# Query norm in the copy of x, attention's sums for two tiles at once, and a reordered schedule, in a fused convolution and linear-attention kernel

## The chip, the core and the metric

The kernel runs on one core of a Trainium2 chip. The metric is the device time of one execution in microseconds (us), the median of several runs. The engines are named as in the profile: PE (matrix products, with PEld for its weight loads), DVE (vector), ACT (scalar), POOL (GpSimd) and SP (the queue that issues the DMAs here). Each engine executes its own instructions in the order in which the program lists them.

## What is computed

There are 16 images x of 256 channels and 64 by 64 pixels, all in float32. For each image:

```python
x = x + conv(gn(x)) * mod        # gn: group norm, 32 groups; conv: 3x3, 8 groups of 32 channels,
                                 # its taps rotated by angles that are computed from the image
t = gn(x)                        # the second norm, as tokens: 4096 x 256
q = t @ Wq.T + bq ; k, v = split(t @ Wkv.T + bkv)
q = (relu(q) + 1e-6) / scale ; k = (relu(k) + 1e-6) / scale
q = q**3 / |q**3| * |q| ; k = k**3 / |k**3| * |k|
z = 1 / (q . sum(k) + 1e-6)                        # 8 heads of 32
out = q @ (k.T @ v) * z + depthwise5x5(v)
x = x + out @ Wproj.T + bproj
```

## The kernel before

**Phases of one image.** The whole order is written out by hand for every engine (a manual schedule). In the key phase (`key_step`, n = 2 to 15 for all but the first image) each step makes 256 tokens' keys and values: `key_products` (PE, L588), `key_bias` (DVE), `squares` (ACT, sums of squares for the focusing norm), `cube` (POOL, L567), `ratio` (DVE) and `root` (POOL, L576), `key_scale` (ACT, L608), and `values`, which adds k.T @ v into PSUM (PE, L621). `key_store` writes the values to DRAM and `load_blocks` reads them back as 12 by 8 blocks (`vh`) for the depthwise convolution. Sixteen such loads fill `vh` for the upper half of the image, the last two being issued after n = 14. `depthwise` (PE `pd`, L658, with ACT copying `pd` into `fm`) needs all sixteen.

`between` is the transition: the first two `query_products` (PE `pq`, L683), the last three `values`, and the depthwise convolution of the upper half.

Then come 17 steps of `attention_step`, p = 1 to 17. In step p, `turn` transposes the queries of group p-1 (PE `pt`, L698; ACT copies `pt` to `qT`, L703), `query_products` makes group p+1, `query_bias` adds bias and relu on DVE (L557, L558), `turn_back` transposes the output of group p-2 (PE `po`, L734; ACT copies it to `oT`), `attend` makes the sums of group p-1 (PE `pn`, L715) and `project` multiplies group p-2 by Wproj (PE `py`, L744). `add_up` (DVE, L756) adds the result to x one step later. On PE a step thus runs `pt`, `pq`, `po`, `pn`, `py`. In `attend` DVE makes the denominators `zz` (L717), inverts them (L720) and multiplies (`o`, L724), and POOL adds the depthwise result (`o`, L726), each for two tiles j = 0, 1 in turn; `po` of the next step reads `o`.

**What is laid over the attention steps.** The next image's 3x3 convolution runs in the same steps: `convolve` (PE `pc`, four PSUM banks) at the end of p = 2, 3, 4 and 9, 10, 11, in parts A, P, B. In the step after it `evict` empties the four banks q = 0 to 3 into x (part A on ACT, P on ACT and DVE, B on DVE). `settle` corrects the edges of x (POOL, L443) and then takes the statistics for the second norm (DVE, L444). The lower half's depthwise convolution is in p = 9. `norm1` is the second norm of the next image, a chain whose links are stepped through one at a time by `next(chain)`: bn_aggr on DVE; `pm` (PE, L196) and four small DVE instructions; `pv` (PE, L203), `vs` (DVE, L205) and a power on POOL (L206); `fold_scale`, which multiplies Wkv by the norm's factor (DVE, L531); `fold_shift`, which subtracts the mean's part from the bias (PE `pbkv`, L538, and DVE). Two links per step are made, from p = 14, one in the middle and one at the end. The next image's first keys are made in p = 16 and 17.

**What sets the order around the change.** Each engine's queue is what is written in these functions. PSUM has six banks in a ring (`bank`, L90): a product waits until the bank taken six before it has been read. Two more banks hold k.T @ v, and later the sums of the two tiles. The tables say in which step something happens:

```python
SETTLES = {4: (0, 0, (0, 1), (2, 3)), 8: (0, 1, (0,), ()), 9: (0, 1, (1, 2), (3,)),
           11: (1, 0, (0, 1), (2, 3)), 13: (1, 1, (0, 1), ()), 14: (1, 1, (2, 3), ())}
```

(step: half, row parity, the quarters settled in the middle of the step, those settled late in it.) Wq is treated as Wkv is: loaded again for each image, scaled by the norm (`fold_scale(b, "q")` at n = 5) and its bias corrected (`fold_shift(b, "q")` at n = 8, PE `pbq`). `blocked` (ACT, L675) copies x into the token order of a query group.

Of the kernel before, what the change touches and what calls it, by code (L numbers as in the profile page):

```python
# [26 lines left out]

STRIP = 2 * ROWS
# [8 lines left out]
SETTLES = {4: (0, 0, (0, 1), (2, 3)), 8: (0, 1, (0,), ()), 9: (0, 1, (1, 2), (3,)),  # L37
           11: (1, 0, (0, 1), (2, 3)), 13: (1, 1, (0, 1), ()), 14: (1, 1, (2, 3), ())}
# [6 lines left out]
STATS = {1: (0,), 2: (1, 2), 3: (3,), 7: (4,), 9: (5, 6), 10: (7,)}  # L45
# [18 lines left out]
def conv_attention(ctx: ExitStack, tc: tile.TileContext, x, consts, kw, b1, w2, b2, b2r,  # L64
# [16 lines left out]
    ps = pool("ps", 6, space=PSUM)  # L81
# [7 lines left out]

    def bank(name):  # L90
        return ps.tile([P, CH], F32, tag="bank", name=name)
# [7 lines left out]
    def load_stats(b, i):  # L99
        if i == 0:  # L100
            state[b] = {"x": {}, "k": {}, "xs": {},
                        "st": sp.tile([P, 2, NCH, 6], F32, tag="st0", name=f"st0_{b}", bufs=1)}

            if b > 1:
                state[b]["xw"] = wsp.tile([P, 2, CH], F32, tag="wkv", name=f"xs_{b}")
        if b > 1:
            xt = state[b]["xw"]
            for t in range(2):
                nc.sync.dma_start(xt[:, t, :], x[b, ts(t, P), ts(i, CH)])
        else:  # L110
            xt = xp.tile([P, 2, CH], F32, tag="x", name=f"xs_{b}_{i}")
            nc.sync.dma_start(xt, halves(x[b])[:, :, ts(i, CH)])
        state[b]["xs"][i] = xt

    def take_stats(b, i):
        xt = state[b]["xs"].pop(i)
        for t in range(2):
            nc.vector.bn_stats(state[b]["st"][:, t, i, :], xt[:, t, :])
# [66 lines left out]
    def gn_coefs(st, b, which):  # L185


        mv = sp.tile([P, 2, 2], F32, tag="mv", name=f"mv{which}_{b}")
        for t in range(2):
            nc.vector.bn_aggr(mv[:, t, :], st[:, t])  # L190
        yield
        mean, var = mv[:, :, 0], mv[:, :, 1]
        co = sp.tile([P, 5, 2], F32, tag=f"co{which}", name=f"co{which}_{b}")
        a, pooled, d, v, m = (co[:, k, :] for k in range(5))
        pm = bank(f"pm{which}_{b}")[:, 0:2]
        nc.tensor.matmul(pm, lhsT=g8, rhs=mean, start=True, stop=True)  # L196
        nc.vector.tensor_copy(m, pm)
        nc.vector.tensor_sub(d, mean, m)
        nc.vector.tensor_mul(v, d, d)
        nc.vector.tensor_add(v, v, var)  # L200
        yield
        pv = bank(f"pv{which}_{b}")[:, 0:2]
        nc.tensor.matmul(pv, lhsT=g8, rhs=v, start=True, stop=True)  # L203
        vs = sp.tile([P, 2], F32, tag="vs", name=f"vs{which}_{b}")
        nc.vector.tensor_scalar(vs, pv, EPS_GN, None, ALU.add)  # L205
        nc.gpsimd.tensor_tensor(a, vs, mhalf, ALU.pow)  # L206
        yield
        if which == 0:
            nc.vector.tensor_mul(pooled, d, a)
        return a, pooled, m  # L210
# [7 lines left out]
    def prepare(b):  # L218
# [15 lines left out]
        nc.vector.tensor_add(h, ph, b1_t)  # L234
        nc.vector.tensor_scalar(h, h, 0.0, None, ALU.max)
# [14 lines left out]
        nc.vector.tensor_add(mod, pmod, b2r_t)  # L250

# [9 lines left out]
        nc.vector.tensor_copy(edge, pe)  # L261
        state[b]["edge"] = edge
# [61 lines left out]
        def shifts(t):  # L324


            pb = bank(f"pbias_{b}_{t}")[:, 0:3]
            for j in range(4):
                for dx in range(3):
                    nc.tensor.matmul(pb[ts(j, HD), dx:dx + 1], lhsT=sums[t][:, dx, :], rhs=gm[:, t, j:j + 1],  # L330
                                     start=True, stop=True, tile_position=(0, HD * j))
            nc.vector.tensor_copy(shift[:, t, 0:3], pb)
            nc.vector.tensor_reduce(shift[:, t, 3:4], shift[:, t, 0:3], AX.X, ALU.add)
            nc.vector.tensor_scalar(shift[:, t, 3:4], shift[:, t, 3:4], -1.0, None, ALU.mult)
# [84 lines left out]
    def evict(b, u, part, q):  # L419

        at, shift = (2 * u + q // 2, q % 2), state[b]["shift"][:, q % 2, 3:4]
        pc = state[b]["pc"][q].rearrange("p (r w) -> p r w", w=W)
        fresh = at not in state[b]["x"]
        if fresh:
            state[b]["x"][at] = xp.tile([P, 2 * CH], F32, tag="x", name=f"x_{b}_{at[0]}_{at[1]}")
        rows = rows_16(b, u, q)
        if part == "P":
            nc.scalar.activation(rows[:, 1], pc, AF.Identity, bias=shift, scale=-1.0)
        if part == "B":
            nc.vector.tensor_add(rows[:, 1], pc, rows[:, 1])  # L430
        elif fresh:
            nc.scalar.activation(rows[:, 0], pc, AF.Identity, bias=shift)
        else:
            nc.vector.tensor_add(rows[:, 0], pc, rows[:, 0])  # L434

# [72 lines left out]
    nc.vector.tensor_add(bp_t, bp_t, pb)  # L508

# [23 lines left out]
    def fold_shift(b, name):  # L533
# [6 lines left out]
        nc.vector.tensor_sub(br, br, pb[:, 0:n])  # L540

    def norm1(b):
        a, _, m = yield from gn_coefs(state[b]["st1"], b, 1)
        state[b]["gn1"] = (a, m)
        fold_scale(b, "kv")
        yield
        fold_shift(b, "kv")
# [44 lines left out]
    def key_bias(b, n, j):  # L592
# [4 lines left out]
        nc.vector.tensor_add(vbuf[n % NV][:, j, 0:HD, :].rearrange("p c h -> p (c h)"), pm[:, C:2 * C], br[:, C:2 * C])  # L597

# [11 lines left out]
    def values(b, n):  # L610


        if n == 0:
            state[b]["pkv"] = [psk.tile([P, HD + 1], F32, tag=f"kv{hh}", name=f"pkv{hh}_{b}") for hh in range(2)]
# [33 lines left out]
    def depthwise(b, half, c):  # L648
# [7 lines left out]
        for k in range(4):  # L656
            for j in range(4):
# [8 lines left out]
                       pd.rearrange("p k (T h) -> p k T h", h=NH))  # L666


    def blocked(b, m):
# [3 lines left out]
        for t in range(2):  # L673
            xt = chunk(b, i, t).rearrange("p (y R J c) -> p R J y c", y=BR, R=2, c=BC)
            nc.scalar.copy(xq[:, t, :].rearrange("p (J y c) -> p J y c", y=BR, c=BC), xt[:, R])  # L675
        state[b]["xq"][m] = xq

    def query_products(b, m):
        xq, (w, _) = state[b]["xq"].pop(m), state[b]["q"]
# [9 lines left out]
    def query_bias(b, m):  # L689
        f = state[b]["f"][m]  # L690
        relu(f["r"], f["pq"], state[b]["q"][1].unsqueeze(1).to_broadcast([P, 2, C]))
# [9 lines left out]
    def turned(b, m):  # L701
        qT = op.tile([P, 2, 2, P], F32, tag="qT", name=f"qT_{b}_{m}", bufs=1)
        nc.scalar.copy(qT, state[b]["pt"])  # L703
        state[b]["qT"] = qT

    def attend(b, m):
# [4 lines left out]
        pns = []  # L711
        for j in range(2):
            pn = psk.tile([P, HD + 1, NH], F32, tag=f"kv{j}", name=f"pn_{b}_{m}_{j}")
            for hh in range(2):
                nc.tensor.matmul(pn[:, :, 4 * hh:4 * hh + 4], lhsT=qT[:, hh, j, :], rhs=kvx[:, hh],  # L715
                                 start=True, stop=True)
            nc.vector.scalar_tensor_tensor(z[:, j, :], factor[:, j:j + 1].to_broadcast([P, NH]), EPS, pn[:, HD, :],  # L717
                                           ALU.mult, ALU.add)
            pns.append(pn)
        nc.vector.reciprocal(z, z)  # L720
        state[b]["o"] = []
        for j in range(2):
            o = op.tile([P, HD, NH], F32, tag="o", name=f"o_{b}_{m}_{j}")
            nc.vector.tensor_mul(o, pns[j][:, 0:HD, :], z[:, j, :].unsqueeze(1).to_broadcast([P, HD, NH]))  # L724
            o = o.rearrange("p c h -> p (c h)")
            nc.gpsimd.tensor_add(o, o, fm[:, 2 * (m % NCH) + j, :])  # L726
            state[b]["o"].append(o)

    def turn_back(b, m):

        po = bank(f"po_{b}_{m}").rearrange("p (t j n) -> p t j n", t=2, j=2)
        for j in range(2):
            for t in range(2):
                nc.tensor.transpose(po[:, t, j, :], state[b]["o"][j][:, ts(t, P)], ident)  # L734
        oT = op.tile([P, 2, 2 * P], F32, tag="oT", name=f"oT_{b}_{m}", bufs=1)
        nc.scalar.copy(oT.rearrange("p t (j n) -> p t j n", j=2), po)  # L736
        state[b]["oT"] = oT
# [14 lines left out]
    def add_up(b, m):  # L752
        i, R = divmod(m, 2)
        for co in range(2):
            xt = chunk(b, i, co).rearrange("p (y R n) -> p R y n", y=BR, R=2)[:, R]
            nc.vector.scalar_tensor_tensor(xt, state[b]["py"][:, co], bp_t[:, co:co + 1], xt, ALU.add, ALU.add)  # L756

# [62 lines left out]
    def between(b, more):  # L820
# [7 lines left out]
        query_bias(b, 0)  # L828
        key_scale(b, NP - 2)
        blocked(b, 2)  # L830
        squares(k[NP - 1], 1)
        for n in range(NP - LATE, NP - 2):
            values(b, n)
        query_products(b, 1)
# [4 lines left out]
        values(b, NP - 2)  # L839
        query_bias(b, 1)  # L840
        for c in range(0, HD // 2, 4):
            depthwise(b, 0, c)
        key_scale(b, NP - 1)
# [10 lines left out]
    def attention_step(b, p, chain):  # L854
# [7 lines left out]
        v, s, early, late = SETTLES.get(p, (0, 0, (), ())) if more else (0, 0, (), ())  # L862
# [3 lines left out]
        if part:  # L866
            evict(b + 1, u, part, 0)
        if p >= 3:
            add_up(b, p - 3)
            store(b, p - 3)  # L870
        if p - 1 < NP:
            turn(b, p - 1)
            turned(b, p - 1)
        if part:
            evict(b + 1, u, part, 1)
# [5 lines left out]
        for q in early:  # L881
            settle(b + 1, v, s, q)
        if chain:
            next(chain, None)
        if p == NP + 1:
            turn_back(b, p - 2)
        if n >= 0:
# [6 lines left out]
            if n >= 1:  # L894
                squares(k[n - 1], 0)
                cube(k[n - 1])
            key_bias(b + 1, n, 0)
            key_bias(b + 1, n, 1)
        if part:
            evict(b + 1, u, part, 2)  # L900
# [9 lines left out]
        for q in late:  # L910
            settle(b + 1, v, s, q)
# [12 lines left out]
        if p >= 2:  # L924
            project(b, p - 2)
        if more and p in SUMS:
# [3 lines left out]
        if chain:  # L930
            next(chain, None)
# [12 lines left out]
    with tc.manual_schedule():  # L944
        fold_load(0, "q")
        made = iter(())
        for b in range(B):
            more = b + 1 < B
            state[b]["f"], state[b]["xq"] = {}, {}
            for n in range(0 if b == 0 else LEAD, NP):  # L950
# [12 lines left out]
                if b > 0 and n == LEAD:  # L963
                    fold_load(b, "q")
                if n == 5:
                    fold_scale(b, "q")
                if n == 8:
                    fold_shift(b, "q")
# [99 lines left out]
```

## Time and profile before

| | |
|---|---|
| median of 3 runs | 3654.27 us (3651.45 to 3654.44) |
| the profiled execution | 3651.46 us, of which its span is 3649.7 us |
| PE busy | 3425.5 us, 94% of the span |
| PEld, DVE, ACT, POOL busy | 71%, 68%, 56%, 56% |
| mean granted PE clock | 0.984 |
| DMA | 505.90 MB, 139 GB/s on average |

All numbers are of one execution. A row of the page or of the groups names the line, the engine, the operation, out<-in with shapes and the count; then the busy time and the mean of one in ns; then the engine's idle time just before these instructions and what ended it. A row of the timeline gives start and length in us, and in brackets the idle time before it and its releaser. Idle time of an engine that isn't the bottleneck costs nothing by itself.

### The profile page before, as it was taken

The numbers are of one execution on the slowest core, as the hardware profiler recorded it, in microseconds if no ns is written. First come the engines' busy times: TensorE is split into PE (matmuls) and PEld (weight loads), VectorE is DVE, ScalarE is ACT, GpSimd is POOL, SyncE is SP. The second block draws the span as 40 slices with busy tenths as digits, with TensorE's granted clock in tenths as the row PEclk, the third lists the DMA queues.
The fourth block names the chain that finished last, engine by engine and source line by source line (L and its number), as shares of the span: only waits on it lengthen the run. The fifth ranks groups of instructions, "written<-read, shape, count | busy, mean of one in ns | idle before, by whom it ended". The sixth has DMA issues, their size and how long they took to land. (4 is left out here: it accounts for less than half of the span.)

```text
span 3649.7 us, 109597 instructions
## 1 busy us (share of the span) xinstructions
PE 3425.5 (94%) x43496; PEld 2580.0 (71%) x43496; DVE 2477.9 (68%) x6627; ACT 2036.9 (56%) x6501; POOL 2034.4 (56%) x2554
## 2 busy tenths in 40 slices
PE   2799999999999999999999999999999999999999
PEld 1467677677777767776677776777777776777778
DVE  4667767667676666766677576776766667676656
ACT  2264654647556465564646546475564755646565
POOL 4265555556555565564655555565555655546545
PEclk8899999999999999999999999999999999999999
DMA  4263552635436253462634526355262534525242
GB/s 138 95 196 102 155 164 76 201 95 171 153 103 203 80 180 122 131 180 82 204 107 154 164 69 209 95 167 158 96 206 85 180 121 139 175 80 182 78 145 99
DMA packets 191173, 505.90 MB, mean 139 GB/s; under 512 B 30742, under 2 KB 103960, under 8 KB 178373
## 3 DMA queue, kind: packets, MB, share of 16 engines
q1 hardware_dynamic: 190660, 498.89, 43.4%
q8 instruction: 344, 5.64, 0.7%
q14 instruction: 169, 1.38, 0.1%
HBM read 363.24 MB, written 135.53 MB: 137 GB/s over the span
## 5 line engine op out<-in xcount | busy, mean ns | idle before, releaser
L588 PE MATMUL pk<-wkv,x 128*128 128x512 f32 x2048 | 951.6, 611 | 0.0
L588 PEld LDWEIGHTS pk<-wkv,x 128*128 128x128 f32 x2048 | 617.5, 310 | 213.2 <-issue 6.1
L726 POOL TENSOR_TENSOR o<-o,fm 128x256 f32<-128x256 f32 x512 | 365.6, 736 | 702.4 <-DVE o L724 445.1
L744 PE MATMUL py<-oT,wp 128*128 128x256 f32 x2048 | 522.3, 399 | 2.7 <-ACT oT L736 2.5
L683 PE MATMUL pq<-wq,xq 128*128 128x256 f32 x2048 | 496.1, 385 | 24.8 <-DVE x L434 24.5
L564 ACT ACTIVATE r_k<-rk 128x256 f32<-128x256 f32 x1024 | 416.2, 407 | 154.4 <-POOL rk L567 93.3
L564 ACT ACTIVATE r_q<-rq 128x256 f32<-128x256 f32 x1024 | 413.4, 407 | 97.1 <-POOL rq L567 95.2
L683 PEld LDWEIGHTS pq<-wq,xq 128*128 128x128 f32 x2048 | 372.1, 192 | 76.4 <-DVE x L434 31.7
L744 PEld LDWEIGHTS py<-oT,wp 128*128 128x128 f32 x2048 | 382.8, 196 | 58.0 <-issue 3.6
L736 ACT COPY oT<-po 128x512 f32<-128x512 f32 x256 | 150.0, 586 | 427.9 <-PE po L734 427.4
L567 POOL TENSOR_TENSOR rk<-r_k,rk 128x512 f32<-128x512 f32 x256 | 328.2, 1282 | 96.6 <-ACT r_k L564 93.1
L576 POOL TENSOR_TENSOR s_k<-s_k,phalf 128x2 f32<-128x2 f32 x256 | 177.1, 692 | 355.6 <-DVE s_k L573 347.2
L608 ACT ACTIVATE rk<-rk,s_k 128x256 f32<-128x256 f32 x512 | 231.5, 499 | 213.0 <-POOL s_k L576 213.0
L384 POOL TENSOR_TENSOR arena<-arena 128x512 f32<-128x512 f32 x244 | 305.8, 1285 | 50.1 <-DMA arena<-in_x 21.0
L567 POOL TENSOR_TENSOR rq<-r_q,rq 128x512 f32<-128x512 f32 x256 | 327.6, 1280 | 0.0
L703 ACT COPY qT<-pt 128x512 f32<-128x512 f32 x256 | 149.0, 582 | 315.5 <-PE pt L698 315.3
L557 DVE TENSOR_TENSOR pq<-pq,bq 128x512 f32<-128x512 f32 x256 | 178.3, 696 | 187.5 <-PE pq L683 183.8
L557 DVE TENSOR_TENSOR pk<-pk,bkv 128x256 f32<-128x256 f32 x512 | 217.8, 425 | 124.0 <-PE pk L588 123.4
L715 PE MATMUL pn<-kvx,qT 128*128 128x132 f32 x2048 | 282.2, 282 | 0.0
L576 POOL TENSOR_TENSOR s_q<-s_q,phalf 128x2 f32<-128x2 f32 x256 | 179.9, 703 | 180.9 <-DVE s_q L573 176.7
L715 PEld LDWEIGHTS pn<-kvx,qT 128*128 128x128 f32 x2048 | 257.4, 195 | 4.4 <-ACT qT L703 3.9
L444 DVE BATCH_NORM_STATS2 st<-x 128x6 f32<-128x512 f32 x256 | 165.3, 683 | 130.9 <-POOL x L443 130.9
(161 smaller groups left out, 5992.6 us busy)
## 6 DMA issues: line engine op xcount, KB each, us to landing
vh<-vpad SPq DMA_DIRECT2D x256, 384.0 KB
vh<-vpad SPq DMA_DIRECT2D x256, 360.0 KB
vpad<-arena SPq DMA_DIRECT2D x512, 128.0 KB
out<-x SPq DMA_DIRECT2D x128, 512.0 KB
xs<-in_x SPq DMA_DIRECT2D x224, 256.0 KB
arena<-in_x SPq DMA_DIRECT2D x248, 144.0 KB
arena<-in_x SPq DMA_DIRECT2D x248, 136.0 KB
xs<-in_x SPq DMA_DIRECT2D x16, 512.0 KB
```

The source lines that it names most:

```text
L384: nc.gpsimd.tensor_add(s[:, j], g[:, j, odd:odd + STRIP:2], g[:, j, even:even + STRIP - 1:2])
L444: nc.vector.bn_stats(state[b]["st1"][:, t, 2 * I + s, :], rows)
L557: nc.vector.tensor_add(pm, pm, bias)
L564: nc.scalar.activation(f["r2"][:, j, :], f["r"][:, j, :], AF.Square, accum_out=f["s"][:, k, j:j + 1])
L567: nc.gpsimd.tensor_mul(f["r"], f["r2"], f["r"])
L576: nc.gpsimd.tensor_tensor(f["s"][:, 3, :], f["s"][:, 2, :], phalf, ALU.pow)
L588: nc.tensor.matmul(pm, lhsT=chunk(b, n // 2, t)[:, T % BC:CH:BC], rhs=w[:, t, :], start=t == 0, stop=t == 1)
L608: nc.scalar.mul(f["r"][:, j, :], f["r"][:, j, :], f["s"][:, 3, j:j + 1])
L683: nc.tensor.matmul(pq[:, j, :], lhsT=xq[:, t, ts(j, P)], rhs=w[:, t, :], start=t == 0, stop=t == 1)
L715: nc.tensor.matmul(pn[:, :, 4 * hh:4 * hh + 4], lhsT=qT[:, hh, j, :], rhs=kvx[:, hh], start=True, stop=True)
L726: nc.gpsimd.tensor_add(o, o, fm[:, 2 * (m % NCH) + j, :])
L744: nc.tensor.matmul(py[:, co].rearrange("p y (J c) -> p J y c", c=BC), lhsT=wp_t[:, t, ts(co, P)], rhs=oT[:, t, :].rearrange("p (J y c) -> ...
```

## The change

1. Wq is loaded once. Its scaling and bias correction per image are dropped, and `blocked` applies the norm while it copies x: an ACT activation with a factor and an offset for each partition in place of a plain copy. `norm1` makes the offset with one more DVE instruction.
2. `attend` makes one PSUM tile of two banks for both tiles j: one DVE instruction for the denominators, one for `o` (128x512), and one POOL addition (128x512).
3. The six banks are handed out from a list: a bank joins its end when its reader is issued (`leave`), and the next product takes the first.
4. `evict` and `settle` stand elsewhere: in parts P and B the first bank is emptied after `add_up`, in part A after `turned`; the banks 1 and 2 after `query_bias`. Quarters are settled at the end of the step in p = 4 and 11, and otherwise all right after `query_bias`, in p = 6, 7, 8 and 13.
5. `norm1` takes its links half a step later: the first at the end of p = 14, then the middle and the end of p = 15, the start of p = 16, and the last after p = 16's key products.
6. In `between` both `query_products` come first, then one `values`, half of the depthwise convolution, the second `values`, the other half, and the last `values`.

```diff
-SETTLES = {4: (0, 0, (0, 1), (2, 3)), 8: (0, 1, (0,), ()), 9: (0, 1, (1, 2), (3,)),
-           11: (1, 0, (0, 1), (2, 3)), 13: (1, 1, (0, 1), ()), 14: (1, 1, (2, 3), ())}
+SETTLES = {4: (0, 0, range(4)), 6: (0, 1, (0, 1)), 7: (0, 1, (2,)), 8: (0, 1, (3,)),
+           11: (1, 0, range(4)), 13: (1, 1, range(4))}
-STATS = {1: (0,), 2: (1, 2), 3: (3,), 7: (4,), 9: (5, 6), 10: (7,)}
+STATS = {1: (0,), 2: (1, 2), 3: (3,), 8: (4,), 9: (5, 6), 10: (7,)}
...
     def bank(name):
-        return ps.tile([P, CH], F32, tag="bank", name=name)
+        held[name] = idle.pop(0)
+        return ps.tile([P, CH], F32, tag=held[name], name=name)
+
+    def leave(name):
+        idle.append(held.pop(name))
...
     def norm1(b):
-        a, _, m = yield from gn_coefs(state[b]["st1"], b, 1)
-        state[b]["gn1"] = (a, m)
+        a, offset, m = yield from gn_coefs(state[b]["st1"], b, 1)
+        nc.vector.scalar_tensor_tensor(offset, m, -1.0, a, ALU.mult, ALU.mult)
+        state[b]["gn1"] = (a, m, offset)
...
-            nc.scalar.copy(xq[:, t, :].rearrange("p (J y c) -> p J y c", y=BR, c=BC), xt[:, R])
+            a, _, offset = (v[:, t:t + 1] for v in state[b]["gn1"])
+            nc.scalar.activation(xq[:, t, :].rearrange("p (J y c) -> p J y c", y=BR, c=BC), xt[:, R],
+                                 AF.Identity, bias=offset, scale=a)
...
-            pn = psk.tile([P, HD + 1, NH], F32, tag=f"kv{j}", name=f"pn_{b}_{m}_{j}")
+        pn = psk.tile([P, 2, CH], F32, tag="kv", name=f"pn_{b}_{m}")
...
+        nc.vector.scalar_tensor_tensor(z, factor.unsqueeze(2).to_broadcast([P, 2, NH]), EPS, pn[:, :, C:C + NH],
+                                       ALU.mult, ALU.add)
         nc.vector.reciprocal(z, z)
...
+        o = op.tile([P, 2, C], F32, tag="o", name=f"o_{b}_{m}", bufs=1)
+        nc.vector.tensor_mul(o.rearrange("p j (c h) -> p j c h", h=NH),
+                             pn[:, :, 0:C].rearrange("p j (c h) -> p j c h", h=NH),
+                             z.unsqueeze(2).to_broadcast([P, 2, HD, NH]))
+        M = 2 * (m % NCH)
+        nc.gpsimd.tensor_add(o, o, fm[:, M:M + 2, :])
...
         query_bias(b, 0)
+        query_products(b, 1)
         key_scale(b, NP - 2)
         blocked(b, 2)
         squares(k[NP - 1], 1)
-        for n in range(NP - LATE, NP - 2):
-            values(b, n)
-        query_products(b, 1)
+        values(b, NP - LATE)
...
-        values(b, NP - 2)
         query_bias(b, 1)
         for c in range(0, HD // 2, 4):
             depthwise(b, 0, c)
+        values(b, NP - 2)
         key_scale(b, NP - 1)
         for c in range(HD // 2, HD, 4):
             depthwise(b, 0, c)
...
+        if chain and p == NP:
+            next(chain)
         if p - 1 < NP:
             ratio(f[p - 1], True)
             root(f[p - 1])
-        if part:
-            evict(b + 1, u, part, 0)
         if p >= 3:
             add_up(b, p - 3)
             store(b, p - 3)
+        if part and part != "A":
+            evict(b + 1, u, part, 0)
         if p - 1 < NP:
             turn(b, p - 1)
             turned(b, p - 1)
-        if part:
-            evict(b + 1, u, part, 1)
+        if part == "A":
+            evict(b + 1, u, part, 0)
...
-        for q in early:
-            settle(b + 1, v, s, q)
-        if chain:
-            next(chain, None)
+        if part:
+            evict(b + 1, u, part, 1)
+            evict(b + 1, u, part, 2)
+        elif p != SECOND:
+            for q in qs:
+                settle(b + 1, v, s, q)
+        if chain and p == NP - 1:
+            next(chain)
...
+            if chain and p == NP:
+                next(chain, None)
             key_bias(b + 1, n, 0)
...
+        if part:
+            for q in qs:
+                settle(b + 1, v, s, q)
...
-        if chain:
-            next(chain, None)
+        if chain and p < NP:
+            next(chain)
...
-                if b > 0 and n == LEAD:
-                    fold_load(b, "q")
-                if n == 5:
-                    fold_scale(b, "q")
-                if n == 8:
-                    fold_shift(b, "q")
```

## The prediction

> **What bounds the kernel now.** I read the page first, then the groups of instructions with their idle times, then the time line of single steps, then busy shares in short windows.
>
> ```profile
> PE 3425.5 (94%) x43496; PEld 2580.0 (71%) x43496; DVE 2477.9 (68%) x6627; ACT 2036.9 (56%) x6501; POOL 2034.4 (56%) x2554
> L683 PE MATMUL pq<-wq,xq 128*128 128x256 f32 x2048 | 496.1, 385 | 24.8 <-DVE x L434 24.5 <-DVE x L430 0.2
> L621 PE MATMUL pkv<-arena,rk 128*32 128x33 f32 x8192 | 174.9, 241 | 30.3 <-ACT rk L608 28.3 <-issue 2.0
> L203 PE MATMUL pv<-co,consts 128*128 128x2 f32 x64 | 11.8, 255 | 27.8 <-DVE co L200 27.8
> L538 PE MATMUL pbq<-wq,co 128*128 128x256 f32 x64 | 16.4, 379 | 0.0
> ```
>
> PE is the bound, and its idle time is small: of an image's 221.6 us it waits 8.5. Split by image, the waits are `pkv` for ACT 1.87, `pq` for an eviction 1.43, `pv` 1.74, `pm` 0.86, `po` about 0.7, a `pc_0B` every other image. The change aims at each of these. But PE is also slowed by its clock:
>
> ```profile
> 3239.55:3242.97 3.42, 1.69 (x15) 1.59 (x15) 2.90 (x11) 1.17 (x2) 2.65 (x4) 1.00 0.03 14
> 3242.97:3246.38 3.41, 3.41 (x10) 2.74 (x9) 3.10 (x8) 0.91 (x4) 2.91 (x4) 0.50 0.00 0
> 2799.24:2802.65 3.41, 2.10 (x16) 2.05 (x17) 2.68 (x11) 0.84 (x2) 2.78 (x4) 1.00 0.00 0
> ```
>
> The columns are window, length, busy time of PE, PEld, DVE, ACT, POOL, then PE's granted clock. The clock's records lie on a grid of 3.413 us. The waits of `pm` and `pv` leave PE idle for half of one window, and in the next the clock is 0.50: `py` goes from 0.22 to 0.43 us a product. With 2.10 us busy (third line) it stays at 1.00. Windows under 0.50 busy were all followed by half clock, those over 0.60 all but once not. The norm's waits cost 17 halved windows in 15 images, 1.71 us of lost work each: 1.9 us an image.
>
> **The handoff.** Each step, `po` waits for `zz`, reciprocal, `o` and POOL's addition of the step before. Steps 13 and 14, with two quarters settled between:
>
> ```profile
> 3229.03 0.70 DVE L557 TENSOR_TENSOR pq<-pq,bq 128x512 f32<-128x512 f32 x1
> 3229.42 1.27 POOL L567 TENSOR_TENSOR rq<-r_q,rq 128x512 f32<-128x512 f32 x1
> 3230.66 0.41 POOL L443 TENSOR_TENSOR x<-x,shift 128x16 f32<-128x16 f32 x2
> 3230.92 1.29 DVE L444 BATCH_NORM_STATS2 st<-x 128x6 f32<-128x512 f32 x2 [0.47 <-POOL x L443]
> 3232.12 0.22 DVE L717 SCALAR_TENSOR_TENSOR zz<-s_q,pn 128x8 f32<-128x8 f32 x2
> 3232.66 0.76 DVE L724 TENSOR_TENSOR o<-pn,zz 128x256 f32<-128x256 f32 x2
> 3233.26 1.41 POOL L726 TENSOR_TENSOR o<-o,fm 128x256 f32<-128x256 f32 x2 [2.19 <-DVE o L724]
> 3234.72 0.44 PE L734 MATMUL po<-consts,o 128*128 128x128 f32 x2 [0.19 <-POOL o L726]
> ```
>
> The settling sits in DVE's queue before `zz`, and its edge correction sits behind POOL's cube, so one settled quarter moves `zz` by 1.2 us, each further one by 0.64. From `zz` to the last addition's end takes 2.55 us, to the first one's 1.86. Merged it is 0.15 (L717) + 0.25 (L720) + 0.69 (a 128x512 on DVE, L557) + 1.28 (a 128x512 on POOL, L567) + 0.25 of gaps = 2.62, and all four `po` wait for it. The spare time from the second addition to `po` is, by group: 4 and 11, 0.25; 5 and 6, 1.47; 12, 0.05 with the wait shown. These are where the new places of `evict` and `settle` fall. All terms are us per image.
>
> **What goes.** `pbq` is 0.9 from start to start on PE. Emptying part P's first bank after `add_up` frees `pq`'s bank in time: 1.43. The `pc_0B` waits, 7.3 us in all, are 0.3. The `pm` and `pv` waits, 2.6, go: half a step lies behind each. Together 5.2. Wq's loads, scaling and its bias subtraction on DVE lie under PE-bound key steps: nothing more.
>
> **What comes, by step.** Part A (p = 3, 10): three evictions follow `qT` on ACT, where the first used to fill ACT's wait for `pt`; `oT` is 0.13 late, and `py` follows `oT` by 0.06: 0.26 for both.
> p = 2: `po` of group 0 already waits on its handoff; undivided, 0.32 more.
> p = 5, 12 (part B): DVE used to empty bank 1 while it waited for `pq` (0.84 idle remained). Now three evictions follow `query_bias`, `zz` is 0.62 later, plus the longer handoff, less the 0.25 spare: `po` waits 0.73 in p = 6 and 0.77 in p = 13.
> p = 6: POOL ends the late addition, copies two edge rows (0.5), root 0.70, cube 1.27, then two corrections; DVE's two statistics end 3.1 us after `query_bias`. `po` of p = 7 waits 1.25 after that. p = 7, one quarter and the same queue: 0.65 in p = 8. p = 8's falls under the depthwise products.
> p = 13: four quarters, 2 x 0.64 more than in the lines above, on top of the late start: `po` of p = 14 waits 2.1 where it waited 0.2: 1.9.
> p = 15: the addition again, 0.25.
> p = 16: the chain of the norm. `pv` is now the last product of p = 15 and only `pt` (0.45) lies between it and `pk`, which needs the scaled Wkv:
>
> ```profile
> 3242.34 0.15 DVE L205 TENSOR_SCALAR vs<-pv 128x2 f32<-128x2 f32 x1
> 3243.61 0.69 POOL L206 TENSOR_TENSOR co<-vs,mhalf 128x2 f32<-128x2 f32 x1
> 3244.37 1.79 DVE L531 TENSOR_SCALAR wkv<-wkv,co 128x512 f32<-128x512 f32 x2
> ```
>
> The power queues behind the addition of group 14, which ends 1.1 us after `pv`; then 0.7, the new offset 0.2, and the first half of Wkv 0.94 (`pbkv` started on that half alone in one image): `pk` waits 2.5. Before, `po`, `pn`, `py` and `pt` stood there.
> p = 17: `pbkv` now follows the key products, so DVE's bias subtraction (0.7) and six key operations (2.3) begin 1.7 later, and `zz` of group 15 is behind them; `po` waits 2.35 for 0.23 before: 2.1.
> Together 0.26 + 0.32 + 2.6 + 2.7 + 0.25 + 2.5 + 2.1 = 10.7.
>
> **The transition.** With both `pq` first, `values` has its scaled keys and the 1.87 wait is gone, but `pd` could start 4.2 us after the first `pq`, and it started 7.5 after. What it then waits for is the sixteen loads of `vh`:
>
> ```profile
> 452.36 1.91 PE L658 MATMUL pd<-vh,band 107*32 107x128 f32 x61 [0.98 <-DMA arena<-in_x]
> 3308.00:3316.00 8.00, 8.00 (x104) 5.60 (x102) 6.87 (x18) 7.31 (x22) 6.10 (x11) 1.00 0.90 264
> ```
>
> Four images already wait 0.6 to 1.0 there. By the DMA packets the last load ends 0.6 to 4.0 us (mean 2.0) before `pd` in images 1 to 14, and the DMA engines are 0.90 busy in that stretch, so it won't land sooner. With 0.75 from landing to start, as the waiting images show, `pd` waits 0.0 to 4.2, mean 2.3, for 1.87 + 0.22 before: 0.2 worse. In image 0 the loads end 12 us early, and 1.9 is saved.
>
> ACT's copy with factor and offset: with one such operand a 128x256 takes 499 ns (L608), without 407 (L564). Two are not in the trace; between 0 and 2 x 0.09 for each of two copies, at most 0.37 a step. ACT waits 1.2 us for `pt` and 1.3 or more for `po` in a short step, which hides it; uncovered it would be 4 an image. I take nothing.
>
> **The sum.** 10.7 + 0.2 - 5.2 = 5.7 an image, 15 times, less 3 for the first and last: 82. The clock: four waits (transition, p = 14, 16, 17) are over half a window, 1.7. Such a wait leaves half a window idle only if the grid lies well; I count one in two, 2 x 1.71 = 3.4 for 1.9 before: 1.5 x 15 = 22. The profiled execution took 3651.5 (span 3649.7), 2.8 under the median: 3651.5 + 82 + 22 = 3756; among medians I put it at 3757. With no halved window it is 3705, with all four 3808.
>
> The Trainium skill ("TensorE: Matmul & The Clock Gate", "Why this matters for your kernels") has the clock fall only after idle gaps of about 3 us, one whole window. Here 0.86 and 1.74, apart, were enough, so the rows decide. By the rule none of the new waits but the longest of the transition would halve it, and the sum would be near 3705.
>
> **Rivals.** *Handoffs half as dear.* The terms that run through the handoff are 0.32 + 2.6 + 2.7 + 0.25 + 2.1 = 8.0. If engines that idle meanwhile catch up by half, 4.0 goes, and two of the four clock places: (1.7 - 0.2) x 15 - 3, 3671. For it: DVE is busy only 68%. Against: the shown wait of p = 14 came out of the same queue to within 0.05.
> *Faster: the handoff has room.* If `zz` to `po` has 1.5 to 2 us of slack that I don't see at these steps, all 8.0 goes, and the change is worth (-2.3 - 0.2) x 15 - 3 = -40: 3611. It decides from the point where 7.2 of the 8.0 is absorbed. For it: spare time of 1.47 in groups 5 and 6. Against: 0.25 and 0.05 in 4, 11 and 12.
> *Nothing moves*: gains and waits cancel, 3654. The norm's move not doing what it says is in the forecast: its wait goes from `pv` to `pk`.
>
> **Numbers.** Forecast 0.69 (own range 3705 to 3808), half as dear 0.17, faster 0.11, nothing 0.03. A difference under 0.2% (7 us) can't be told here. So faster 0.11, same 0.03, slower 0.86. The range takes in the half case with a few us below it: 3665 to 3808.
>
> **What would show it.** Right: `pq` waits for L434 and the `pv` wait gone; `po` waits for POOL growing from 12 to over 100 us in all, in p = 7, 14 and 17; `pk` waiting for the scaling some 2.5 an image; `pd` waiting for a DMA, 2 an image; more halved windows. Wrong: `po` waits as before, or `pd` starting 4.2 us after `pq` without a wait.

## The result

The changed kernel takes 3789.57 us (median of 4 runs, 3787.51 to 3795.63), the kernel before 3652.86 in the same runs: ratio 1.0383, 95% interval [1.0361, 1.0405]. Slower, 33 us more so than forecast, inside the range. The profiled execution took 3789.39 us, its span is 3787.6 and the mean granted PE clock 0.971 (before 0.984). Of all executions behind this document one, of the combined version below, took 6653.15 us; that version's ratio leaves it out, its median of ten does not.

The page's line of engines, then from the groups of PE two rows of before that the prediction does not show, and the rows that changed:

```profile
PE 3457.4 (91%) x43432; PEld 2571.7 (68%) x43432; DVE 2455.4 (65%) x6083; ACT 2117.0 (56%) x6501; POOL 1992.4 (53%) x2298
```
```profile
L734 PE MATMUL po<-consts,o 128*128 128x128 f32 x1024 | 169.9, 281 | 11.9 <-POOL o L726 11.6
L588 PE MATMUL pk<-wkv,x 128*128 128x512 f32 x2048 | 951.6, 611 | 0.0
```
```profile
L759 PE MATMUL po<-consts,o 128*128 128x128 f32 x1024 | 165.9, 286 | 120.1 <-POOL o L751 120.1
L607 PE MATMUL pk<-wkv,x 128*128 128x512 f32 x2048 | 991.3, 634 | 34.3 <-issue 34.3
L707 PE MATMUL pq<-wq,xq 128*128 128x256 f32 x2048 | 504.0, 392 | 39.7 <-DVE x L782 37.1 <-ACT x L447 2.5
L679 PE MATMUL pd<-vh,band 107*32 107x128 f32 x8192 | 249.0, 280 | 33.6 <-DMA vpad<-arena 9.3 <-issue 7.2 <-DMA arena<-in_x 4.9
L642 PE MATMUL pkv<-arena,rk 128*32 128x33 f32 x8192 | 176.3, 241 | 9.9 <-ACT rk L628 6.4 <-issue 3.2
L213 PE MATMUL pv<-co,consts 128*128 128x2 f32 x64 | 9.7, 221 | 0.9 <-DVE co L210 0.9
```

The last columns are the idle time of PE before the group and what ended it. `po` went from 11.9 to 120.1 us, `pk` from 0 to 34.3, `pv` from 27.8 to 0.9; the wait of `pq` for L434 (24.5) is gone. All of that was forecast. The row of `pk` names no releaser ("issue"); the time line of one image shows what it waits for:

```profile
1993.29 0.70 POOL L217 TENSOR_TENSOR co<-vs,mhalf 128x2 f32<-128x2 f32 x1
1994.10 0.88 DVE L548 TENSOR_SCALAR wkv<-wkv,co 128x512 f32<-128x512 f32 x2
1994.68 3.79 PE L607 MATMUL pk<-wkv,x 128*128 128x512 f32 x8 [2.29 <-issue]
```

The 0.88 us are two instructions, one for each half of Wkv. In all 15 images the first `pk` starts 0.10 us after the first of them ends.

The 37.1 us in which `pq` waits for L782, `add_up`, were not forecast. PE is busy 32 us longer although `pbq` (16.4) is gone, and `pk` is now 634 ns a product where it was 611: that is the clock, which stands at 0.50 after the wait of `pk` in 14 images.

The sum of the idle columns over all groups of PE is 219 us before and 325 after, 106 more. Halved clock windows (3.413 us at 0.50, counted in the clock's records after the first 250 us) went from 20 to 47; at 1.71 us each these are 46 more. Less `pbq`'s 16 that makes 136, and the span grew by 138. By the wait that fills most of PE's idle time in the window before, 14 of the 47 follow `pk`, 11 `pq` in p = 3, 9 `po` in p = 17 and 5 `pd`; 6 are second windows of a longer halved stretch, and 2 follow other waits.

The unforeseen wait, in the time line of step p = 3 of one image:

```profile
2101.41 1.27 DVE L127 BATCH_NORM_STATS2 st<-xs 128x6 f32<-128x512 f32 x2
2102.12 9.34 SPq L117 DMA_DIRECT2D xs<-in_x  x4
2109.32 0.70 DVE L127 BATCH_NORM_STATS2 st<-xs 128x6 f32<-128x512 f32 x1 [6.64 <-DMA xs<-in_x]
2111.35 0.87 DVE L782 SCALAR_TENSOR_TENSOR x<-py,bp,x 128x256 f32<-128x256 f32 x2
2112.36 3.63 PE L707 MATMUL pq<-wq,xq 128*128 128x256 f32 x8 [4.78 <-DVE x L782]
```

In p = 2 DVE takes two statistics of the image after next (table STATS). The second one's load is issued only when the first has freed the buffer, and DVE waits 6.64 us for it. `add_up` of group 0 stands behind it in DVE's queue, and the list of banks now gives `pq` the bank that this `add_up` empties. In the kernel before DVE waited as long (7.52 at 2032.46), with `add_up` at 2034.02, but `pq` had started at 2029.32, in another bank. What follows the wait, in windows of the clock's grid (the first two of the four; the other two are at `pk` in another image; the columns are as before, PE's busy time first, its clock behind POOL):

```profile
2108.92:2112.33 3.41, 0.00 (x0) 0.00 (x0) 2.40 (x6) 1.08 (x2) 0.82 (x2) 1.00 0.26 85
2112.33:2115.74 3.41, 3.38 (x8) 2.75 (x9) 0.00 (x0) 0.00 (x0) 1.11 (x1) 0.50 0.80 249
2221.56:2224.97 3.41, 1.13 (x6) 0.80 (x6) 1.86 (x9) 0.59 (x1) 1.92 (x2) 1.00 0.00 0
2224.97:2228.38 3.41, 3.41 (x6) 1.33 (x5) 0.78 (x2) 0.00 (x0) 0.69 (x1) 0.50 0.02 5
```

### The profile page after: what moved, and what is told of

It is laid out like the page before. It is cut to its first block, busy times and chain, and to the rows that moved or that the text cites. A ratio compares the mean times of both kernels' runs of the same rounds, so it can differ in the third digit from the quotient of the medians.

```text
span 3787.6 us, 108421 instructions
## 1 busy us (share of the span) xinstructions
PE 3457.4 (91%) x43432; PEld 2571.7 (68%) x43432; DVE 2455.4 (65%) x6083; ACT 2117.0 (56%) x6501; POOL 1992.4 (53%) x2298
## 3 DMA queue, kind: packets, MB, share of 16 engines
q1 hardware_dynamic: 184420, 492.99, 40.8%
## 5 line engine op out<-in xcount | busy, mean ns | idle before, releaser
L607 PE MATMUL pk<-wkv,x 128*128 128x512 f32 x2048 | 991.3, 634 | 34.3 <-issue 34.3
L751 POOL TENSOR_TENSOR o<-o,fm 128x512 f32<-128x512 f32 x256 | 326.7, 1276 | 895.2 <-DVE o L747 388.3
L707 PE MATMUL pq<-wq,xq 128*128 128x256 f32 x2048 | 504.0, 392 | 39.7 <-DVE x L782 37.1
L770 PE MATMUL py<-oT,wp 128*128 128x256 f32 x2048 | 505.3, 389 | 0.9 <-ACT oT L761 0.7
L707 PEld LDWEIGHTS pq<-wq,xq 128*128 128x128 f32 x2048 | 381.2, 196 | 89.9 <-issue 21.4
L770 PEld LDWEIGHTS py<-oT,wp 128*128 128x128 f32 x2048 | 369.4, 190 | 52.3 <-issue 3.6
L628 ACT ACTIVATE rk<-rk,s_k 128x256 f32<-128x256 f32 x512 | 231.7, 500 | 203.6 <-POOL s_k L595 203.6
L679 PE MATMUL pd<-vh,band 107*32 107x128 f32 x8192 | 249.0, 280 | 33.6 <-DMA vpad<-arena 9.3
L698 ACT ACTIVATE xq<-x,co 128x256 f32<-128x256 f32 x512 | 279.2, 596 | 0.0
```

The costliest lines, as they stand in the source:

```text
L607: nc.tensor.matmul(pm, lhsT=chunk(b, n // 2, t)[:, T % BC:CH:BC], rhs=w[:, t, :], start=t == 0, stop=t == 1)
L679: nc.tensor.matmul(pd[ts(j, HD), k, :].rearrange("p (R m h) -> p R m h", R=4, m=4), lhsT=band_t[:, c + k, :], rhs=vb[:, :, :, j, c + k, :] ...
L698: nc.scalar.activation(xq[:, t, :].rearrange("p (J y c) -> p J y c", y=BR, c=BC), xt[:, R], AF.Identity, bias=offset, scale=a)
L707: nc.tensor.matmul(pq[:, j, :], lhsT=xq[:, t, ts(j, P)], rhs=w[:, t, :], start=t == 0, stop=t == 1)
L751: nc.gpsimd.tensor_add(o, o, fm[:, M:M + 2, :])
L770: nc.tensor.matmul(py[:, co].rearrange("p y (J c) -> p J y c", c=BC), lhsT=wp_t[:, t, ts(co, P)], rhs=oT[:, t, :].rearrange("p (J y c) -> ...
```

## The experiments

Each row is the median of its runs and its ratio to the kernel before in the same runs; PE's idle sum and the halved windows are counted as above, in the profiled execution, which can lie off the median: 15 us above it with two tiles apart, 15 below it with evict and settle as before. "Changed" and "before" name the kernel that was edited.

| kernel | us | ratio, 95% | PE idle | halved |
|---|---|---|---|---|
| before | 3652.86 | 1 | 219 | 20 |
| changed | 3789.57 | 1.0383 [1.0361, 1.0405] | 325 | 47 |
| changed, ring of banks | 3721.12 | 1.0184 [1.0146, 1.0222] | 304 | 19 |
| changed, one statistic a step | 3721.51 | 1.0182 [1.0149, 1.0215] | 285 | 23 |
| changed, evict and settle as before | 3727.6 | 1.0194 [1.0157, 1.0231] | 282 | 24 |
| changed, norm's links as before | 3705.74 | 1.0142 [1.0108, 1.0175] | 279 | 22 |
| changed, ring and norm's links | 3662.29 | 1.0025 [1.0009, 1.0042] | 263 | 12 |
| changed, two tiles apart | 3770.77 | 1.0335 [1.0307, 1.0363] | 303 | 46 |
| changed, transition as before | 3795.92 | 1.0398 [1.0378, 1.0418] | 338 | 45 |
| before, query norm alone | 3656.6 | 1.0004 [0.9987, 1.002] | 238 | 15 |
| combined | 3642.23 | 0.9971 [0.9953, 0.9989] | 239 | 8 |
| combined, merged tiles | 3638.51 | 0.9972 [0.9959, 0.9986] | 249 | 4 |
| before, settled in p = 13 | 3616.64 | 0.9918 [0.9889, 0.9947] | 208 | 2 |
| the same, part P as changed | 3591.3 | 0.9827 [0.9803, 0.9852] | 188 | 5 |

**The list of banks.** Two kernels take the same wait away by different means: the ring gives `pq` another bank, the other keeps the bank and takes DVE's wait for the load away.

```diff
-    ps = pool("ps", 1, space=PSUM)
+    ps = pool("ps", BANKS, space=PSUM)
...
-        held[name] = idle.pop(0)
-        return ps.tile([P, CH], F32, tag=held[name], name=name)
+        return ps.tile([P, CH], F32, tag="bank", name=name)
...
```


> Changed kernel, with the ring of six banks in place of the list; all else is unchanged. Theory A (the list is a cost that the forecast didn't have): with the list pq of p = 3 gets the bank of py and waits for add_up, which DVE reaches only after statistics that wait for a load of x; with the ring pq, po and py of p = 3 have other banks and only the third bank of the convolution waits for add_up. Wait of pq for add_up (37.1 us) gone, and with its halved windows 4.4 us in each of 13 images: 3725 to 3750 us. Theory B (DVE is late for po and the convolution all the same): the wait only moves to po, pc or the next pq, and under 15 us is saved: 3775 to 3792.


```diff
-STATS = {1: (0,), 2: (1, 2), 3: (3,), 8: (4,), 9: (5, 6), 10: (7,)}
+STATS = {1: (0,), 2: (1,), 3: (2,), 5: (3,), 8: (4,), 9: (5, 6), 10: (7,)}
```


> Changed kernel, with the list of banks, but one statistic less in p = 2: the chunks of the image after next are taken in p = 1, 2, 3, 5 in place of 1, 2, 2, 3, so that each load has a step or more to land. Theory A: DVE no longer waits for the load ahead of add_up, and pq of p = 3 no longer waits, though it has the same bank: 3725 to 3750 us, as with the ring. Theory B (the bank list itself, not DVE's wait for the load, makes the step long): 3775 to 3792.

Both are 68 us faster than the changed kernel, a little below theory A's range; theory B falls. The rows of `pq` and `pk` with the ring (line numbers are one lower):

```profile
L706 PE MATMUL pq<-wq,xq 128*128 128x256 f32 x2048 | 489.1, 383 | 10.9 <-ACT qT L727 10.2 <-DVE x L781 0.7
L606 PE MATMUL pk<-wkv,x 128*128 128x512 f32 x2048 | 976.1, 626 | 33.3 <-DVE wkv L547 33.3
```

Of the 37.1 us 0.7 is left, and 28 halved windows are gone, 48 us. Not all of these are the price of this wait: the 11 after `pq` and five of the six second windows are gone, but so are 10 of the 14 after `pk`, which waits as long as before (33.3 for 34.3). Whether a wait of 2.3 us halves the next window depends on how it falls on the clock's grid, and that moved. With one statistic a step five of those 14 went. The idle sum falls by 21 only, since the ring brings waits of the first image back (11 us net) and `pq` now waits 10.2 for `qT`; here `pk`'s releaser is named, the scaling of Wkv. With one statistic a step the idle sum falls by 40.

**Places of evict and settle.**

```diff
-SETTLES = {4: (0, 0, range(4)), 6: (0, 1, (0, 1)), 7: (0, 1, (2,)), 8: (0, 1, (3,)),
-           11: (1, 0, range(4)), 13: (1, 1, range(4))}
+SETTLES = {4: (0, 0, (0, 1), (2, 3)), 8: (0, 1, (0,), ()), 9: (0, 1, (1, 2), (3,)),
+           11: (1, 0, (0, 1), (2, 3)), 13: (1, 1, (0, 1), ()), 14: (1, 1, (2, 3), ())}
...
+        if part:
+            evict(b + 1, u, part, 0)
         if p >= 3:
             add_up(b, p - 3)
...
```


> Changed kernel, with the places of evict and settle (and the one statistic that moved with them) as before. Forecast's theory: the waits of po in p = 6, 7, 8, 13, 14 and 15 fall from 4.6 us an image to about 0.6, the wait of pq for the evicted bank of part P (1.4) comes back, and pq of p = 3 gets a bank that is free (po then waits for add_up): 4.5 us an image, with one halved window in two at p = 14, 70 to 85 us less: 3705 to 3725. Rival (handoffs half as dear): 25 to 40 us less: 3750 to 3765.

It came out 62 us faster: 8 less than the forecast's range, and well over the rival's (25 to 40). The time alone decides little, because the run also takes the wait of `pq` for `add_up` (37.1) away. The row of `po` does: its wait for POOL fell from 120.1 to 63.5, 3.8 us an image, where the forecast says 4.0 and the rival half of that. In return `po` waits 17.2 for `add_up`, `pq` again 21.5 for part P, and `pm` 20.7 for what is queued ahead of the norm.

**The norm's links.**

```diff
-        if chain and p == NP:
-            next(chain)
...
-        if chain and p == NP - 1:
-            next(chain)
+        if chain:
+            next(chain, None)
...
-            if chain and p == NP:
-                next(chain, None)
...
-        if chain and p < NP:
-            next(chain)
+        if chain:
+            next(chain, None)
```


> Changed kernel, with the links of the second norm where they were before. Forecast's theory: the waits of pk for the scaled Wkv (2.3) and of po of group 15 (2.2) go, those of pm and pv (2.6) come back, and the halved windows are the same number: 1.9 us an image, 15 to 45 us less: 3745 to 3775. Rival (the move is neutral, as pm and pv bring back as much): 3782 to 3795.

84 us faster, far more than either expected. From the groups of that kernel:

```profile
L759 PE MATMUL po<-consts,o 128*128 128x128 f32 x1024 | 164.6, 284 | 88.5 <-POOL o L751 88.5
L607 PE MATMUL pk<-wkv,x 128*128 128x512 f32 x2048 | 949.4, 612 | 0.0
L213 PE MATMUL pv<-co,consts 128*128 128x2 f32 x64 | 10.8, 238 | 15.5 <-DVE s_q L591 14.6 <-DVE co L210 0.9
L205 PE MATMUL pm<-mv,consts 128*128 128x2 f32 x64 | 9.8, 223 | 26.7 <-DVE mv L199 26.7
```

`pk`'s 34.3 and 31.6 of `po`'s wait are gone, but `pm` does not wait at all (26.7 is the first image's, and also stands in the rows of before) and `pv` 1.0 an image. Before, the two together waited 2.6. With the links where they were, 1.6 of the forecast's 2.6 stays gained; the next run shows that the settling in p = 13 brings it. The half step between the links brings 1.0 and costs 2.3 at `pk`, 2.1 at `po` and the halved windows there. 45 us of idle time and 25 halved windows (43) make up the difference.

The settling was tried by itself, with one line of the kernel before:

```diff
-           11: (1, 0, (0, 1), (2, 3)), 13: (1, 1, (0, 1), ()), 14: (1, 1, (2, 3), ())}
+           11: (1, 0, (0, 1), (2, 3)), 13: (1, 1, (0, 1), (2, 3))}
```


> Kernel before, with only the last two quarters settled late in p = 13 in place of the middle of p = 14; the norm's links stay. Theory (the wait of pm and pv comes from the two quarters settled just ahead of the norm, not from the norm's own places): pm and pv fall from 2.6 us an image to 1.5 or less and the halved window after them (1.7) goes, for 1.2 more at po of p = 14: 1.0 to 2.5 us an image, 3615 to 3638 us. Forecast's view (the half step between the links is what is missing): pm and pv wait as before and po waits 1.2 more: 3660 to 3675.


```profile
L203 PE MATMUL pv<-co,consts 128*128 128x2 f32 x64 | 11.2, 245 | 14.6 <-DVE co L200 14.6
L196 PE MATMUL pm<-mv,consts 128*128 128x2 f32 x64 | 9.8, 223 | 26.5 <-DVE mv L190 26.5
L734 PE MATMUL po<-consts,o 128*128 128x128 f32 x1024 | 168.7, 280 | 26.2 <-POOL o L726 25.8
```

`pm` loses the 12.9 that it waited for L717, `pv` falls from 27.8 to 14.6, `po` pays 14.3, and the halved windows fall from 20 to 2: 3616.64. Theory and range hold, and the forecast's view falls. The idle sum is only 10 us lower; the rest of the gain is the 18 windows (31 us).

**Are they two waits or one?** The ring and the norm's links together:

> Changed kernel, with both the ring of banks and the norm's links in their former places. If these are two separate waits (p = 3; p = 14 to 17), their gains of 69 and 84 us add: 3790 - 153 = 3637, 3625 to 3650 us, under the kernel before. If they share one cause (a clock that each of them alone restores: the mean clock was 0.984 and 0.982 with one of them, 0.971 without), little comes on top of the larger: 3680 to 3705.

127 of the 153 us: between the two ranges, nearer to two separate waits. PE's idle sum falls by 62, nearly the 21 and 46 of the two alone. The halved windows fall by 35, 18 fewer than the 28 and 25 of the two alone, and these 18 (31 us) are about what is lacking to 153. Ten of them stood after `pk`: the ring alone had already taken them, and the norm's links take the wait itself. What is left of the change without these two parts is 0.25% slower than before: its `po` waits 89 us and `pd` 42, against gains at `pq`, `pm`, `pv` and `pkv`.

**Sums for both tiles.** `attend` as before, the rest as changed (`pn`, `zz`, `o` and POOL's addition for each j).

> Changed kernel, with attention's sums, o and its addition for each tile in turn, as before. Forecast's terms: the first tile's addition ends 0.7 us earlier and two of the four po (0.44) run while the second ends, in the 7 or 8 places where po waits: 0.4 to 0.5 each, 3 to 4 us an image, 45 to 60 us less: 3730 to 3745. Rival (the last addition decides, and it ends within 0.07 of the same time): 3783 to 3792.

```profile
L759 PE MATMUL po<-consts,o 128*128 128x128 f32 x1024 | 188.6, 289 | 75.7 <-POOL o L751 75.4
```

`po` waits 44.4 us less (120.1 to 75.7), as expected, but the time fell by only 19, between the two expectations. Half of the gain goes back to `po` itself: PE is busy with it for 22.7 us more (188.6 for 165.9), since two pairs take 0.44 us each where four products in a row take 0.60 to 0.66. `pd` waited 12 more and `pq` 8, and the halved windows stayed (46). The merging costs, by less than half of what was expected.

**The transition.** `between` as before.

> Changed kernel, with the order of between as before. Forecast: either order waits for the sixteen loads of vh, 0.2 us an image: 3780 to 3795 us. Rival (the wait of pd, 33.6 us in all here against 9.9 before, is the new order's own and halves windows too): 1.0 to 2.5 us an image, 15 to 40 us less: 3750 to 3775.

```profile
L679 PE MATMUL pd<-vh,band 107*32 107x128 f32 x8192 | 237.2, 273 | 10.1 <-issue 8.4 <-DVE x L782 0.4 <-PE pkv L642 0.2
L642 PE MATMUL pkv<-arena,rk 128*32 128x33 f32 x8192 | 180.6, 241 | 40.8 <-ACT rk L628 38.8 <-issue 1.6
```

The median is 6 us above the changed kernel's, a difference that the two intervals don't separate, and 1 above the forecast's range; the rival's time falls. Its first half holds, however: the wait of `pd` is the new order's own. With the order of before `pd` waits 10.1 us, and PE waits for ACT at `pkv` instead (40.8): together 50.9 for 43.5. The DMA packets of `vh` agree. In images 1 to 14 the last one ended 1.8 to 3.9 us before `pd` here; in the changed kernel `pd` starts 0.6 to 1.1 us after it in 12 of the 14. So the new order gains 31 us at `pkv` and loses 24 at `pd`.

**The query norm alone**, on the kernel before: the copy with factor and offset in `blocked`, and no `fold_load`, `fold_scale` and `fold_shift` for "q".

> Kernel before, with only the query norm in the copy of x (Wq loaded once). Forecast: pbq's 0.9 us an image goes and the longer copies lie under ACT's waits: 14 us less than before, 3633 to 3646 us. Rival (ACT has no room): the two copies of a step take 1.09 us for 0.71 in the trace of the changed kernel; uncovered in 16 steps that is 6 us an image, up to 90 us more, and any part of it shows as waits for xq, qT or oT: 3660 to 3740.

No gain: 11 us above the forecast's range and 3 below the rival's. `pbq` is gone, but (the groups of this kernel; before, 30.3 and 7.3):

```profile
L622 PE MATMUL pkv<-arena,rk 128*32 128x33 f32 x8192 | 180.1, 241 | 39.1 <-ACT rk L609 38.8
L405 PE MATMUL pc_0B<-arena,wt 32*32 32x504 f32 (+1 forms) x2976 | 113.1, 604 | 12.3 <-DVE x L434 12.3
```

ACT is on the path in the transition: its longer copies make the scaled keys late for `pkv` by 0.6 an image; the changed kernel with `between` as before shows the same (40.8). They also bring `pc_0B`'s wait into every image. Together with `pbkv` (3.2 more) that is 17 us more of waits, as much as `pbq` took.

**Put together.** The main lines of the diff, against the kernel with the ring and the norm's links of before; the merged form leaves `attend` as changed:

```diff
+SETTLES = {4: (0, 0, range(4)), 9: (0, 1, range(4)),
+           11: (1, 0, range(4)), 12: (1, 1, (0, 1)), 13: (1, 1, (2, 3))}
+STATS = {1: (0,), 2: (1,), 3: (2,), 5: (3,), 8: (4,), 9: (5, 6), 10: (7,)}
...
+        if part == "B":
+            evict(b + 1, u, part, 0)
         if p >= 3:
             add_up(b, p - 3)
...
```


> A version put together from the runs: changed kernel with the ring of banks, the norm's links and the attention by single tiles as before; one statistic of the image after next per step in p = 1, 2, 3, 5; part B evicted as before, parts A and P as in the change; the second row parity of the first half settled in p = 9 (the depthwise step) and that of the second half by two quarters at the end of p = 12 and two in p = 13. From the waits of po that ring and norm places leave (5.8 us an image): p = 7 and 8 lose 1.5, p = 6 and 13 1.0, p = 14 about 1.0, p = 2 and 17 0.9: 4.4 us an image, 66 us: 3662 - 66 = 3596, 3580 to 3620 us. Rival (the settled quarters only move their wait to pm, pv or the next pq): 3640 to 3660.

> The combined version, but with attention's sums for both tiles at once, as in the change. Forecast's view of that part (all four po wait for the one addition): where po still waits it costs 0.3 to 0.5, with three or four such places 1 to 2 us an image: 15 to 30 us more than the combined version. Rival (fewer instructions on DVE and POOL are a gain where nothing waits): equal or up to 15 us less.

3642 and 3639. The first lies in the rival's range: of `po`'s 89 us 26 are left, as meant, but the waits moved, if not to the places that the rival named alone: `py` waits 18 for `oT`, `pt` 11 for POOL, and `pbkv` 8 and `pq` 7 more than with the ring and the norm's links alone. The merged form is not slower, as its rival said: `po` waits 27 longer, but PE's idle sum grows by 10 only, four halved windows are gone, and the two ratios can't be told apart. In this schedule the merging costs nothing that can be measured.

The simplest version was the better one: the settling in p = 13 and part P's banks emptied as in the change, all else as before.

```diff
+        if part and part != "P":
+            evict(b + 1, u, part, 0)
         if p >= 3:
             add_up(b, p - 3)
             store(b, p - 3)
+        if part == "P":
+            evict(b + 1, u, part, 0)
...
             query_bias(b, p + 1)
+        if part == "P":
+            evict(b + 1, u, part, 1)
+            evict(b + 1, u, part, 2)
...
```


> Kernel before, with the last two quarters settled late in p = 13 (as in the run before) and part P's banks emptied as in the change: the first after add_up, banks 1 and 2 after query_bias. Forecast's term: pq no longer waits for the emptied bank in p = 4 and 11, 1.43 us an image (24.0 us in all in the trace of the run with the settling alone), and the steps shorten from 10.2 and 9.8 us to 8.8: 3617 - 21 to 36: 3581 to 3596 us. Rival (the wait moves on: the evictions behind query_bias make zz late, or pq waits for add_up): 3610 to 3625.


```profile
L683 PE MATMUL pq<-wq,xq 128*128 128x256 f32 x2048 | 494.0, 384 | 9.5 <-DVE x L756 8.1 <-ACT x L428 1.4
```

3591.3, ratio 0.983: 1.7% faster than before. `pq`'s wait fell by 14.6 us, and most of what is left now ends with `add_up` (8.1), as the rival said in part; `pc_0B` waits 4.4 less.

## Why the prediction was right, and where not

**Right in direction and place.** The waits that it named are there, but for part A's: `po` for POOL, `pk` for the scaled Wkv, `pd` for the loads, more halved windows. Those that it said would go went, `pkv`'s for the most part; `pc_0B`'s came back in the first image alone (21.1 of its 21.4 us).

**The handoff**, forecast 8.0 us an image with all its terms, measured 108 us, 7.2. By step, the added waits of `po`: p = 2, 0.53 (0.32); p = 6 to 8 together 2.0 (2.6); p = 13 and 14, 1.9 (2.7); p = 15, 0.47 (0.25); p = 17, 2.2 (2.1). From `zz` to the addition's end took 2.5 to 2.7 in most steps (2.62). So what was too large is the lateness of `zz`: by 0.2 in each of p = 6, 7, 8 and 13, and by 0.5 in p = 14. Why isn't shown. Half as dear was wrong.

**`pk`** waited 2.29 (2.5). The transition's sum came out as forecast, `pd` and `pkv` together 40.2 before and 43.5 after, 0.2 an image; that is luck in part, for both terms were 0.5 too large: `pkv` lost 1.4 of the 1.87, and `pd` gained 1.6 where 2.1 was forecast. **Part A**'s 0.26 isn't there: `py` waits 0.9 in all. `pq`'s wait for part P (1.43 in most images) and `pm` and `pv`'s 2.6 went.

**The first step that failed: part 3 was costed at nothing.** The list of banks was told in the change and had no term in the sum. It made DVE's wait for a load, which was in the trace of before and cost nothing there, PE's wait: 37 us of idle time. Without it the kernel is 68 us faster, halved windows included.

**The second: the clock's term**, 22 us forecast, 46 measured. At the four places named it had counted one in two, 30 windows in 15 images, and 28 came: 14 at p = 16, 9 at p = 17, 5 in the transition and none at p = 14. So the sum was right and its parts were not, which is luck. The excess is the place that it had left out: 11 windows after the wait in p = 3, and second windows (6, where before had 3).

**The third did no harm to the number but was a wrong reason**: the 2.6 of `pm` and `pv` was put down to the half step between the links. The runs show the two quarters settled just before the norm as the cause of 1.6 of it; only the other 1.0 is the half step's. Moved by themselves the two quarters make the kernel before 1% faster.

**ACT's longer copies** were taken as hidden. In the changed kernel that holds (`pkv` waits less than before); with the old order of the transition it doesn't, as the query norm alone showed: 0.6 an image at `pkv`. That lies between the nothing that was forecast and the 4 of copies that nothing hides.

So the forecast was too low by 33 us because of the bank's 37 and 24 more for the clock. The smaller handoff and part A (16), 5 us less of waits in the first 250 us, and 3 each at `pk` and `pbq` took back about half of it.

The clock's rule, weighed again. Over the 14 profiled executions, from 250 us on, the windows at full clock by PE's busy share, and how many were followed by half clock: under 0.40, all 146; 0.40 to 0.50, 79 of 114; 0.50 to 0.60, 10 of 180; over 0.60, 1 of 13356. So the prediction's "under 0.50 all" was too sharp: it held in the trace of before alone. In a window that is halved already the border lies higher: under 0.80 busy, all 29 were followed by another halved one; 0.80 to 0.90, 6 of 15; over 0.90, 6 of 232. The Trainium skill ("TensorE: Matmul & The Clock Gate", "Why this matters for your kernels") asks only that no idle gap be longer than about 3 us. The runs don't agree: in the third of the windows above the longest gap was 2.29 us and PE was busy for 1.13, and the next window was halved.

## What to carry to other kernels

Cost a wait on a clock-gated engine by what it does to its window: here taking 37 us of waits away saved 68, and one table entry that took away only 0.7 us of idle time an image saved 1%, because 18 halved windows went with it. Some of such a gain is luck: 10 of the 28 windows that went with the 37 us stood after another wait, which stayed. When buffers are handed out in another order, list for each product whose reader now frees its buffer and what that reader is queued behind: a stall that was harmless on DVE came onto PE that way. Before a chain is moved away from a wait, look at what is queued ahead of it; moving two settled quarters gained 36 us, and putting the chain back in its place gained 84 in the changed kernel.

## What the hardware showed that was not expected

An ACT activation of 128x256 takes 406 ns as a copy, 500 with one operand per partition (L628) and 596 with two (L698): 95 ns for each, the upper end of what the prediction allowed. A load that is issued when its buffer comes free kept DVE waiting for 6.6 to 7.5 us in p = 2 to 3, and with the same loads one a step `pq` no longer waited for `add_up`. A halved window can hold the clock down for a second one even when PE is busy for 0.80 of it or more (12 of 247).
